# Graph attention on one core: data kept in the queries' order, and the tile of one-edge queries without q

## The chip, the cores and the metric

The kernel runs on one core of one Trainium2 chip. The time is device time in microseconds of that core, from runs of the whole program. A profiled execution, recorded separately, gives the span from the first to the last instruction and what each engine did. Engines are named as in the profile: PE (matmuls), PEld (weight loads of PE), DVE (vector), ACT (scalar), POOL (GpSimd), SP (sync). Gathers and scatters by rows are issued by POOL, plain loads and stores mostly by SP.

## The reference, cut to what matters

Sixteen batches of x (1024 x 512) go through one layer: masked attention with 8 heads of 64 over a fixed adjacency (1024 x 1024, the same in all batches), output projection, residual and layer norm. All is float32.

```
q, k, v = x @ Wq + bq, x @ Wk + bk, x @ Wv + bv        # 8 heads of 64
scores  = q . k / 8 + (1 - adj) * -1e9
attn    = softmax(scores)
out     = (attn @ v) @ Wo + bo
x       = layernorm(x + out)                            # no scale, no shift
```

The adjacency is sparse. A query with no edge gets the mean of all rows of v, since all its scores are shifted alike. A query with exactly one edge has a softmax over one key: its weight is 1, and its attention is that key's row of v.

## The kernel before

**Order by degree.** The function ranks counts the edges of every query, ranks the queries by that count (L395, eight comparisons of 128 x 1024) and scatters (query, count) to a DRAM table, order, by eight row scatters (scatter, L389). SP reads the table back as ranked; asked_row (L409) is the list of original query numbers in sorted order. Sorted queries form eight tiles of 128. The function edges then gathers each tile's rows of the adjacency (codes, L433), multiplies them by the key's number (L438, place), and takes the largest entries out as lists of keys (kl). From these it writes key_row: for each block, one key per query.

**Blocks.** Tile t has OWN[t] blocks in which each of its 128 queries has a key of its own, and BLOCKS[t] blocks that hold the remaining edges of its dense queries, summed by a matmul (add_up). There are NB = 29 + 6 = 35 blocks a batch, 560 in all.

**Fronts.** The products of x with the weights are called fronts: load_x brings a tile of x in (L548, on SP, three tiles ahead, three buffers), transpose_x turns it on PE (pxT, L555), pair projects two tiles to q (pq, four matmuls by product, L584) and to k and v by a scheme of seven products (x, pp, z, L698). All is kept in the natural order of rows: out_q (L614) scales q on DVE and stores it to q_rows, send stores k and v to kv_rows. Both tables exist three times, so that the batches in work do not meet.

**The attention of a block.** gather (L888 on) fetches q rows once per tile (qt, L894) and for the dense blocks qg (L904), and for each block the rows of k and v of its keys (kvg, L910, 128 rows of 4 KB), all by row gathers on POOL. products (L931) multiplies q by k on DVE, scores (L935) sums per head, exponentials (L945) is on ACT, weigh scales v, on ACT (L955, eight instructions) or on DVE (L959), add_own (L971) adds up, normalise (L999, L1000) divides, and the result is transposed on PE (poT, L1008). finish multiplies by Wo (po, L584), adds the residual row gathered from x (y, L752), normalises (a power on POOL, L820) and scatters the rows to their places in the output (L830).

**The order of the work** is written out by hand. A loop runs over steps n, one block each; step n issues products(n+4), exponentials(n+3), the gathers of block n+8, the weighting of a later block and so on, in a fixed order for every engine's queue. Functions given to later(k, ...) are issued k steps on. In each step PE also gets a share of fronts or of finish, by its costs (PRODUCT, SUM, TRANSPOSE), so that the fronts run more than a batch ahead. Thirty-four steps of lead-in come before block 0; in them ranks and edges run beside the fronts of batch 0 and 1. The attended rows of tiles 102 to 111 (SPILL) are stored and multiplied at the end. PSUM has four rotating banks (fill_psum) for pq, pxT, pp, po and poT.

A guard computes whether the assumptions on the counts and on the size of the scores hold; if not, tile_general runs the whole layer again.

Of the kernel before, what the change touches and what calls it, by code (L numbers as in the profile page):

```python
# [26 lines left out]
OWN = (1, 2, 2, 3, 4, 5, 5, 7)  # L27
# [4 lines left out]
KG_BUFS, Q_BUFS, PV_BUFS, Y_BUFS = 8, 7, 5, 6  # L32
NO_ROW = 65536.0

# [7 lines left out]
ROWS = 3  # L42
# [118 lines left out]
def kernel(  # L161
# [48 lines left out]
    own = [sum(OWN[:t]) for t in range(NT)]  # L210

# [17 lines left out]
    with ExitStack() as main:  # L229
# [16 lines left out]
        place = one.tile([P, N], F32, name="place")  # L246
        nc.gpsimd.iota(place, pattern=[[1, N]], base=1, channel_multiplier=0, allow_small_or_imprecise_dtypes=True)
# [15 lines left out]
        key_row = one.tile([P, NB], I32, name="key_row")  # L263
        query_row = one.tile([P, NS], I32, name="query_row")
# [9 lines left out]
        key, rank = (one.tile([P, NT], F32, name=name) for name in ("key", "rank"))  # L274
        rank_row, asked_row = (one.tile([P, NT], I32, name=name) for name in ("rank_row", "asked_row"))
        ADJ = []
# [12 lines left out]
        bias_rows = one.tile([2 * NPAIR, P], F32, name="bias_rows")  # L289
        bv_rows = one.tile([NPAIR, P], F32, name="bv_rows")  # L290

        def loads():
# [14 lines left out]
            for i in range(ROWS):  # L307
                nc.scalar.dma_start(kv_rows[i][N:N + 1, 0:D], zero)
            nc.vector.tensor_scalar(before, place[:, 0:P], -1.0, query[:, 0:1], op0=OP.add, op1=OP.is_gt)
# [40 lines left out]
        now, plan, rest, urgent = [0], {}, {}, []  # L350
# [9 lines left out]
        def ranks():  # L360
# [4 lines left out]
            zeros = small.tile([P, 2 * NT], F32, name="order_first", bufs=1)  # L365
            nc.gpsimd.memset(zeros, 0.0)
            nc.gpsimd.dma_start(order.rearrange("(p t) c -> p (t c)", p=P), zeros)
# [26 lines left out]
            for t in range(NT):  # L394
                nc.vector.scalar_tensor_tensor(  # L395
                    keys, row, key[:, t:t + 1], place, op0=OP.is_lt, op1=OP.min, accum_out=rank[:, t:t + 1]
                )
                if t:
                    nc.vector.tensor_copy(rank_row[:, t - 1:t], rank[:, t - 1:t])
                    scatter(t - 1)  # L400
                if t % 3 == 2:
                    yield
            nc.vector.tensor_copy(rank_row[:, NT - 1:NT], rank[:, NT - 1:NT])
            scatter(NT - 1)
            yield
            nc.sync.dma_start(ranked, order.rearrange("(t p) c -> p t c", p=P))
            yield
            yield
            nc.vector.tensor_copy(asked_row, ranked[:, :, 0])  # L409
            yield  # L410
            nc.vector.tensor_scalar(lone, ranked[:, 0, 1:2], 0.0, None, op0=OP.is_le)
# [16 lines left out]

        def edges(t):
# [8 lines left out]
            nc.vector.tensor_tensor(v, v, place, op=OP.mult)  # L438
            st = small.tile([P, 4], F32, name="est")
            deg, end, lim, off = (st[:, i:i + 1] for i in range(4))  # L440
            kl = small.tile([P, J + 2], F32, tag=f"kl{J}", name=f"kl_{t}", bufs=2 if J == 8 else 1)
            kr = small.tile([P, max(OWN)], F32, tag="kr", name=f"kr_{t}", bufs=2)
# [21 lines left out]
            if J > SEGMENT:  # L464
# [5 lines left out]
            nc.vector.tensor_scalar(off, kl[:, 0:1], 0.0, N + 1.0, op0=OP.is_le, op1=OP.mult)  # L470
            nc.vector.tensor_tensor(kl[:, 0:1], kl[:, 0:1], off, op=OP.add)

            rows, missing = kr[:, 0:K], absent[:, own[t]:own[t] + K]
            nc.vector.tensor_scalar(rows, kl[:, 0:K], -1.0, float(N), op0=OP.add, op1=OP.min)
            nc.vector.tensor_scalar(missing, rows, 0.0, None, op0=OP.is_lt)
            yield
            nc.vector.scalar_tensor_tensor(
                key_row[:, NS + own[t]:NS + own[t] + K], missing, NO_ROW, rows, op0=OP.mult, op1=OP.max
            )
# [13 lines left out]
            nc.vector.tensor_copy(kl[:, J + 1:J + 2], ranked[:, t, 0:1])  # L493
            nc.vector.tensor_tensor(end, off, deg, op=OP.add)
# [10 lines left out]
            step = min(nb, HALF // (J + 2))  # L505
            assert step * J <= D
            for i0 in range(0, nb, step):
# [3 lines left out]
                g = pg[:, 0:n * (J + 2)].rearrange("p (n j) -> p n j", n=n)  # L511
# [3 lines left out]
                e = small.tile([P, 2, n], F32, tag=f"ee{n}", name=f"ee_{t}_{i0}", bufs=2)  # L515
# [11 lines left out]
                nc.vector.tensor_tensor(key_row[:, g0:g0 + n], e[:, 1, :], e[:, 0, :], op=OP.max)  # L527
                nc.vector.tensor_copy(query_row[:, g0:g0 + n], g[:, :, J + 1])
# [16 lines left out]
        def load_x(b, t):  # L545
            if b < B:
                X[b, t] = work.tile([P, D], F32, tag="x", name=f"x_{b}_{t}", bufs=3)
                nc.sync.dma_start(X[b, t], x[b, ds(t * P, P), :])  # L548

        def transpose_x(b, t):  # L550
# [25 lines left out]
            return [(TRANSPOSE, pe, None)]  # L576

        def product(name, lhs, w, out):

            def unit(c):  # L580
# [3 lines left out]
                nc.tensor.matmul(p, lhs()[:, ts(c, P)], w[:, c, :], start=(c == 0), stop=(c == NPAIR - 1))  # L584
# [16 lines left out]
        def pair(b, j):  # L601
# [8 lines left out]
            def out_q(i, p):  # L610

                assert gathered[0] >= NB * (b - ROWS + 1)
# [44 lines left out]
            def lhs(i):  # L657
                return lambda: XT[b, tt[i]]

            q0, q1 = (product(f"pq_{b}_{tt[i]}", lhs(i), W["q"], lambda p, i=i: out_q(i, p)) for i in range(2))  # L660
# [118 lines left out]
        def finish(b, t):  # L779
# [92 lines left out]
            units = product(f"po_{b}_{t}", lambda: OT[b, t], W["o"], out)  # L872
# [10 lines left out]


        KG, QG, PV, PSUM, QT, RDEN = {}, {}, {}, {}, {}, {}
        blocks = [(b, t, i) for b in range(B) for t in range(NT) for i in range(OWN[t] + BLOCKS[t])]

        def gather(n):  # L888
            b, t, i = blocks[n]
# [326 lines left out]
```

## Time and profile before

| what | value |
|---|---|
| median of 3 runs | 1974.01 us (1973.77 to 1976.46) |
| span of the profiled execution | 1981.3 us |
| the profiled execution's own time | not given beside its span |
| busy PE, DVE, ACT, POOL | 1914.7, 1786.6, 1554.5, 1288.2 us |
| DMA | 563.10 MB, mean 284 GB/s |
| row gathers and scatters (software queue) | 403.22 MB, 61.9% of 16 engines' span |
| plain transfers of SP and ACT (main queue) | 153.16 MB, 20.9% |

Busy time of PE is the sum of records that overlap a little, so it is read together with the chain of waits. The chain goes back from the last instruction, at each step to whatever released it. A stage is a stretch of the span, given with the busy time of every engine in it. The groups give count, busy time and mean length per line; "idle before" names what ended the idle time of that engine.

### The profile page before, as it was taken

The page shows a single profiled execution, that of the slowest core. Times are in us where ns is not written, and L with a number is a line of the kernel's source. Part 1 is how long each engine was busy: PE and PEld are TensorE (multiplying, and loading weights), DVE is VectorE, ACT ScalarE, POOL GpSimd, SP SyncE. Part 2 cuts the span into 40 slices and gives each one's busy share as a digit, 9 for nine tenths or more (in the row PEclk, how much of TensorE's full clock was granted, in tenths as well). Part 3 has the DMA queues.
Part 4 walks back from the last instruction along what each step waited for, and adds up shares of the span by engine and source line. Part 5 has one row for each costly group of instructions (what it writes and reads, how often), then busy time and mean ns, then how long its engine had stood idle before and what let it go on. Part 6 is the DMA issues. An engine that isn't in the chain of part 4 may idle for free.

```text
span 1981.3 us, 25750 instructions
## 1 busy us (share of the span) xinstructions
PE 1914.7 (97%) x5375; PEld 923.3 (47%) x5375; DVE 1786.6 (90%) x3756; ACT 1554.5 (78%) x6096; POOL 1288.2 (65%) x1206
## 2 busy tenths in 40 slices
PE   8988999999999999999999999999999999999895
PEld 3434454444545454454544445454444545444442
DVE  2789999999899999999998999989899999999895
ACT  3525878878797887879888787879789798978785
POOL 1653565756667676767667586766757675566684
PEclk9999999999999999999999999999999999999998
DMA  6697887888879788888889788888978889998994
GB/s 250 214 339 253 265 303 246 301 280 273 315 262 318 253 303 287 299 296 270 306 255 319 269 290 285 298 303 262 312 260 290 293 291 321 313 316 269 324 313 154
DMA packets 191140, 563.10 MB, mean 284 GB/s; under 512 B 31711, under 2 KB 31739, under 8 KB 190974
## 3 DMA queue, kind: packets, MB, share of 16 engines
q0 software_dynamic: 121632, 403.22, 61.9%
q1 hardware_dynamic: 66736, 153.16, 20.9%
q10 hardware_dynamic: 2606, 4.99, 0.7%
q14 instruction: 122, 1.00, 0.2%
q8 instruction: 44, 0.72, 0.1%
HBM read 442.25 MB, written 143.71 MB: 296 GB/s over the span
## 4 chain that ended last, share of the span: by engine, by line
PE 75%; DVE 12%; issue 3%; ACT 2%; DMA 0%; POOL 0%; another core or an unknown queue 0%; DVEq 0%; POOLq 0%; ACTq 0%
PE po L584 19%; PE pq L584 17%; PE pp L698 13%; PE z L698 9%; PE x L698 9%; DVE qk L931 3%; DVE s L935 2%; PE poT L1008 2%; PE pxT L555 2%; PE sum L981 2%; PE sum L980 2%; ACT pv L955 1%; DVE pv L971 1%; PE pm L646 1%; DVE o L1000 1%
## 5 line engine op out<-in xcount | busy, mean ns | idle before, releaser
L910 POOL DMA_INDIRECT kvg<-kv_rows,key_row x560 | 629.5, 1124 | 435.0 <-ACT pv L945 111.6
L955 ACT ACTIVATE pv<-kvg,pv 128x64 f32<-128x64 f32 x3552 | 894.4, 338 | 0.0
L584 PE MATMUL pq<-wq,xT 128*128 128x512 f32 x1024 | 481.5, 600 | 2.0 <-issue 1.5
L584 PE MATMUL po<-wo,oT 128*128 128x512 f32 x944 | 436.7, 595 | 4.2 <-DVE y L804 1.9
L935 DVE TENSOR_REDUCE s<-qk 128x8 f32<-128x512 f32 x560 | 380.8, 680 | 6.0
L931 DVE TENSOR_TENSOR qk<-qt,kvg 128x512 f32<-128x512 f32 x464 | 317.4, 684 | 4.8 <-DMA kvg<-kv_rows,key_row 3.1
L584 PEld LDWEIGHTS pq<-wq,xT 128*128 128x128 f32 x1024 | 192.7, 193 | 223.2 <-issue 209.4
L584 PEld LDWEIGHTS po<-wo,oT 128*128 128x128 f32 x944 | 175.5, 191 | 206.1 <-issue 190.8
L698 PE MATMUL pp<-t,s 128*128 128x512 f32 x504 | 239.6, 598 | 9.5 <-DVE s L570 9.5
L698 PE MATMUL x<-b,xT 128*128 128x512 f32 x504 | 237.1, 593 | 0.0
L971 DVE TENSOR_TENSOR pv<-pv,pv 128x520 f32<-128x520 f32 x336 | 232.9, 693 | 0.0
L945 ACT ACTIVATE pv<-s,absent 128x8 f32<-128x8 f32 x464 | 135.3, 293 | 107.7 <-DVE s L935 69.2
L830 POOL DMA_INDIRECT out_dram<-y,asked_row x128 | 153.2, 1197 | 37.6 <-issue 26.1
L894 POOL DMA_INDIRECT qt<-q_rows,asked_row x128 | 139.8, 1092 | 36.8 <-issue 35.0
L594 ACT ACTIVATE sq_k<-kv 128x128 f32<-128x128 f32 x512 | 150.6, 299 | 10.0 <-DVE kv L721 9.0
L698 PEld LDWEIGHTS pp<-t,s 128*128 128x128 f32 x504 | 95.2, 191 | 119.1 <-issue 107.7
L698 PEld LDWEIGHTS x<-b,xT 128*128 128x128 f32 x504 | 94.6, 190 | 112.4 <-issue 109.0
L752 POOL DMA_INDIRECT y<-in_x_dram,asked_row x102 | 116.0, 1137 | 30.6 <-issue 30.0
L904 POOL DMA_INDIRECT qg<-q_rows,query_row x96 | 106.1, 1105 | 27.2 <-issue 25.3
L698 PE MATMUL z<-b,s 128*128 128x512 f32 x252 | 118.5, 592 | 0.7 <-DVE kv L726 0.7
L698 PE MATMUL pp<-t,xT 128*128 128x512 f32 x252 | 118.5, 593 | 0.1
L698 PE MATMUL z<-t,s 128*128 128x512 f32 x252 | 118.6, 593 | 0.0
(195 smaller groups left out, 2608.8 us busy)
## 6 DMA issues: line engine op xcount, KB each, us to landing
kv_rows<-kv SPq DMA_DIRECT2D x128, 512.0 KB
x<-in_x_dram SPq DMA_DIRECT2D x128, 256.0 KB
q_rows<-q SPq DMA_DIRECT2D x128, 256.0 KB
kvg<-kv_rows,key_row POOLq DMA_INDIRECT x560
residual<-y_sorted SPq DMA_DIRECT2D x26, 256.0 KB
y<-residual SPq DMA_DIRECT2D x26, 256.0 KB
adj<-in_adj_dram POOLq DMA_DIRECT2D x8, 512.0 KB
spill<-oT SPq DMA_DIRECT2D x10, 256.0 KB
```

The costliest lines, as they stand in the source:

```text
L584: nc.tensor.matmul(p, lhs()[:, ts(c, P)], w[:, c, :], start=(c == 0), stop=(c == NPAIR - 1))
L594: nc.scalar.activation(sq, s[:, ts(h, P)], AF.Square, scale=scale, accum_out=sums[:, h:h + 1])
L698: nc.tensor.matmul(R[bank], l[:, ts(c, P)], right[:, c, :], start=(first and c == 0), stop=(c == 1), skip_group_check=True,)
L752: nc.gpsimd.indirect_dma_start(out=y, out_offset=None, in_=x_rows, in_offset=bass.IndirectOffsetOnAxis(ap=asked_row[:, t:t + 1], axis=0), ...
L830: nc.gpsimd.indirect_dma_start(out=out_rows[b, t], out_offset=bass.IndirectOffsetOnAxis(ap=asked_row[:, t:t + 1], axis=0), in_=y, in_offse ...
L894: nc.gpsimd.indirect_dma_start(out=QT[b, t], out_offset=None, in_=q_rows[b % ROWS], in_offset=bass.IndirectOffsetOnAxis(ap=asked_row[:, t: ...
L910: nc.gpsimd.indirect_dma_start(out=KG[n], out_offset=None, in_=kv_rows[b % ROWS], in_offset=bass.IndirectOffsetOnAxis(ap=key_row[:, g:g + ...
L931: nc.vector.tensor_tensor(QK[n], q, KG[n][:, 0:D], op=OP.mult)
L935: nc.vector.tensor_reduce(S[n], QK.pop(n).rearrange("p (h d) -> p h d", d=HD), axis=AX.X, op=OP.add)
L945: nc.scalar.activation(PV[n][:, D:], S.pop(n), AF.Exp, bias=bias)
L955: nc.scalar.activation(pv[:, ts(h, HD)], v[:, ds(D + h * HD, HD)], AF.Copy, scale=pv[:, D + h:D + h + 1])
L971: nc.vector.tensor_tensor(PV[b, t], PV[b, t], pv, op=OP.add)
```

## The change

The sorted order, until now only that of the attention, becomes the order of all tables from batch 1 on. load_x gathers the rows of x by asked_row on POOL instead of loading them on SP; so k, v and q of batches 1 to 15 are stored sorted, and a tile of q is read back by a plain load on SP. Batch 0 is projected in the natural order, as the order is not known in time, and has index lists of its own (key_row0, query_row0). As the keys are sorted as well, the lists need each key's sorted place: the multiplier of the adjacency rows is a code (2048 times the place, plus the number), made by ranks from the ranks and spread over the partitions by eight more transposes on PE. decode takes it apart again by four small operations.

The ranks are moved: places 64 to 191 become tile 1, the places below 64 and those from 192 to 255 become tile 0. In the adjacency given, 60 queries have no edge and 141 have one, so tile 1 holds queries with exactly one edge. It has no block: its single key's row of v is gathered (v1, half as wide as kvg) and goes to the transpose in place of the normalised sum. Tile 0 now has two blocks, so there are 28 + 6 = 34 blocks for a batch in which steps are counted (NBT), 544 in all. For batches 1 to 15 no q is projected for tile 1. Buffers move: seven qt buffers become four (qg and v1) and three (qs, for tiles of q).

```diff
-OWN = (1, 2, 2, 3, 4, 5, 5, 7)
+OWN = (2, 1, 2, 3, 4, 5, 5, 7)
...
-KG_BUFS, Q_BUFS, PV_BUFS, Y_BUFS = 8, 7, 5, 6
+KG_BUFS, Q_BUFS, QT_BUFS, PV_BUFS, Y_BUFS = 8, 4, 3, 5, 6
+CODE, ROUND = 2048.0, 12582912.0
+LONE, ONE_KEY = 64, 1
...
             for t in range(NT):
                 nc.vector.scalar_tensor_tensor(
-                    keys, row, key[:, t:t + 1], place, op0=OP.is_lt, op1=OP.min, accum_out=rank[:, t:t + 1]
+                    keys, row, key[:, t:t + 1], place[:, 0:1].to_broadcast([P, N]), op0=OP.is_lt, op1=OP.min, accum_out=rank[:, t:t + 1]
                 )
-                if t:
-                    nc.vector.tensor_copy(rank_row[:, t - 1:t], rank[:, t - 1:t])
-                    scatter(t - 1)
                 if t % 3 == 2:
                     yield
-            nc.vector.tensor_copy(rank_row[:, NT - 1:NT], rank[:, NT - 1:NT])
-            scatter(NT - 1)
+            for at, by in ((LONE, LONE), (LONE + P, -LONE - P), (2 * P, P)):
+                nc.vector.tensor_scalar(key, rank, float(at), float(by), op0=OP.is_ge, op1=OP.mult)
...
+            nc.vector.tensor_tensor(rank, rank, moved, op=OP.add)
+            nc.vector.tensor_copy(rank_row, rank)
+            for t in range(NT):
+                scatter(t)
             yield
             nc.sync.dma_start(ranked, order.rearrange("(t p) c -> p t c", p=P))
...
+            nc.vector.scalar_tensor_tensor(key, rank, CODE, key, op0=OP.mult, op1=OP.add)
+            nc.vector.tensor_copy(keys.rearrange("p (t q) -> p t q", t=NT), key[:, :, None].to_broadcast([P, NT, P]))
+            yield
+            pk = [fill_psum(f"pcodes_{i}") for i in range(2)]
+            for t in range(NT):
+                nc.tensor.matmul(pk[t // 4][:, ts(t % 4, P)], keys[:, ts(t, P)], ident, start=True, stop=True)
...
+                nc.scalar.copy(CODE_OF[i], pk[i])
             nc.vector.tensor_copy(asked_row, ranked[:, :, 0])
             yield
+            known.append(True)
...
+        def decode(code, high):
+            nc.vector.tensor_scalar(high, code, 0.5 - CODE / 2, 1.0 / CODE, op0=OP.add, op1=OP.mult)
+            nc.vector.tensor_scalar(high, high, ROUND, None, op0=OP.add)
+            nc.vector.tensor_scalar(high, high, -ROUND, None, op0=OP.add)
+            nc.vector.scalar_tensor_tensor(code, high, -CODE, code, op0=OP.mult, op1=OP.add)
...
-            nc.vector.tensor_tensor(v, v, place, op=OP.mult)
+            for i in range(2):
+                nc.vector.tensor_tensor(v[:, ts(i, HALF)], v[:, ts(i, HALF)], CODE_OF[i], op=OP.mult)
...
+            decode(rows, high)
+            nc.vector.scalar_tensor_tensor(key_row[:, g:g + K], missing, NO_ROW, high, op0=OP.mult, op1=OP.max)
+            nc.vector.scalar_tensor_tensor(key_row0[:, g:g + K], missing, NO_ROW, rows, op0=OP.mult, op1=OP.max)
...
         def load_x(b, t):
             if b < B:
+                if b and not known:
+                    waiting.append((b, t))
+                    return
                 X[b, t] = work.tile([P, D], F32, tag="x", name=f"x_{b}_{t}", bufs=3)
-                nc.sync.dma_start(X[b, t], x[b, ds(t * P, P), :])
+                if b:
+                    gather_x(X[b, t], b, t)
+                else:
+                    nc.sync.dma_start(X[b, t], x[b, ds(t * P, P), :])
...
+            q0, q1 = (
+                product(f"pq_{b}_{tt[i]}", lhs(i), W["q"], lambda p, i=i: out_q(i, p)) if b == 0 or tt[i] != ONE_KEY else []
+                for i in range(2)
+            )
...
-        blocks = [(b, t, i) for b in range(B) for t in range(NT) for i in range(OWN[t] + BLOCKS[t])]
+        blocks = [(b, t, i) for b in range(B) for t in range(NT) if t != ONE_KEY for i in range(OWN[t] + BLOCKS[t])]
...
         def gather(n):
             b, t, i = blocks[n]
+            if t == ONE_KEY + 1 and i == 0:
+                g = NS + own[ONE_KEY]
+                V1[b] = work.tile([P, D], F32, tag="qt", name=f"v1_{b}", bufs=Q_BUFS)
+                nc.gpsimd.indirect_dma_start(
+                    out=V1[b], out_offset=None, in_=kv_rows[b % ROWS],
+                    in_offset=bass.IndirectOffsetOnAxis(ap=keys_of(b)[:, g:g + 1], axis=0), element_offset=D,
+                )
             if i == 0:
-                tag, bufs = ("qt", Q_BUFS) if fronts or t % 2 else ("x", 3)
+                tag, bufs = ("qs", QT_BUFS) if fronts or t % 2 else ("x", 3)
                 QT[b, t] = work.tile([P, D], F32, tag=tag, name=f"qt_{b}_{t}", bufs=bufs)
-                nc.gpsimd.indirect_dma_start(
-                    out=QT[b, t], out_offset=None, in_=q_rows[b % ROWS],
-                    in_offset=bass.IndirectOffsetOnAxis(ap=asked_row[:, t:t + 1], axis=0),
-                )
+                if b:
+                    nc.sync.dma_start(QT[b, t], q_rows[b % ROWS][ds(t * P, P), :])
+                else:
+                    gather_q(QT[b, t], b, asked_row[:, t:t + 1])
...
-            return 0 < i < OWN[t] or n < total - NB and (n % 2 == 0 or n < NB // 2)
+            return 0 < i < OWN[t] or n < total - NBT and (n % 2 == 0 or n < NBT // 2)
...
+                if 0 <= n < total and blocks[n][1:] == (ONE_KEY + 1, 1):
+                    turn(blocks[n][0], ONE_KEY, V1.pop(blocks[n][0]))
```

For the two tiles with dense queries (6 and 7) the lists of the shared blocks get the same decoding and a second set of query numbers. The new function turn is the former end of normalise: transpose, copy and hand-over. Elsewhere NB becomes NBT, and place shrinks to 640 columns.

## The prediction

> **What bounds the kernel now.** I read the page first, then the stages, then the chain, since an average hides which engine binds where.
>
> ```profile
> span 1981.3 us, 25750 instructions
> ...
> PE 1914.7 (97%) x5375; PEld 923.3 (47%) x5375; DVE 1786.6 (90%) x3756; ACT 1554.5 (78%) x6096; POOL 1288.2 (65%) x1206
> ```
>
> ```profile
> 100.00:150.00 50.00, 43.45 (x109) 18.73 (x108) 43.33 (x124) 11.89 (x50) 29.68 (x29) 0.97 0.96 341
> 150.00:200.00 50.00, 43.87 (x129) 21.17 (x128) 45.80 (x110) 29.92 (x121) 15.37 (x16) 0.93 0.73 253
> ...
> 500.00:1000.00 500.00, 499.02 (x1422) 243.94 (x1422) 467.64 (x958) 412.33 (x1645) 348.76 (x320) 1.00 0.86 290
> ...
> 1700.00:1800.00 100.00, 90.86 (x260) 43.80 (x260) 98.14 (x185) 85.45 (x358) 60.99 (x55) 0.98 0.89 306
> ```
>
> In the stages, the columns after the length are busy time of PE, PEld, DVE, ACT and POOL, then clock, DMA share, GB/s. In mid-run PE has no gap and DVE has 6.5% to spare. From 1700 us it turns round: DVE 98, PE 91. From 100 to 200 us neither is full; each waits for the other. A busy PE alone proves little, so the chain of work from 500 to 1000 us, and three of its pieces:
>
> ```profile
> by line: PE pq L584 23.2%; PE po L584 22.7%; PE pp L698 17.2%; PE z L698 11.3%; PE x L698 11.3%; PE poT L1008 3.1%; PE pxT L555 2.8%; PE sum L981 2.2%; PE sum L980 2.2%; DMA kvg<-kv_rows,key_row 1.9%; PE pm L646 0.8%; issue 0.3%; DVE s L935
> ...
> 556.86 3.43 PE pq L584 x8
> 562.01 3.43 PE po L584 x8
> 571.03 3.43 PE po L584 x8
> ```
>
> The chain is PE for about 97%, so a product taken off PE here is time off the run. The price of a q tile is the piece: eight records, 3.43 us (0.43 us each), not the 600 ns mean of its row. The mean of a batch: the first and last mean L646 start at 117.6 and 1843.9 us, 15 batches, 115.1 us each.
>
> **What the Trainium skill says.** "Perfetto Trace Analysis", Identifying the Most-Contended Engine: matmul busy time misjudges PE, because matmuls are pipelined. The trace agrees: rows of 600 ns follow each other every 430 ns. The same page, DMA Instruction, SWDGE: the record of a GpSimd DMA ends when its descriptors are made, not when the data is there. It agrees: the kvg record takes 1.12 us, while a kvg transfer stands in the chain with 9.36 us. "DMA: Bandwidth & Descriptors", Issuing engines are not separate DMA queues: transfers from SP and POOL share the same 16 engines. So swapping plain and gathered loads between these queues buys no bandwidth. "VectorE: DVE Perf Modes", the errata section: each SBUF operation pays a fixed latency, so small ones are dear. Here 128x1 takes 145 ns (L817) against 682 ns for 128x512.
>
> **The change part by part.**
>
> 1. *No q for tile 1 in batches 1 to 15.* Fifteen products of 3.43 us leave PE, 51.5 us in all. Batches 2 to 14 are projected while PE binds, which counts in full: 13 x 3.43 = 44.6. Batch 1's falls in the DVE-paced set-up (0.6 us, its DVE part), batch 15's after 1727 us (the last-but-one mean), where DVE binds. DVE loses 15 q of 0.68, SP 15 stores.
>
> 2. *One block fewer per batch* (35 to 34; tile 0 takes two, tile 1 none). DVE loses per batch the product 0.684, the score 0.680, one weighting (0.686; seven to six by the parity rule), the reciprocal 0.193, the scaling o 0.694; with q 0.682 that is 3.62 us. ACT loses one exponential (0.29); its 28 weightings stay. DVE goes from 107.7 (0.936 x 115.1) to 104.1 of the new 111.7 us: it keeps the same slack, and PE remains the bound. Where DVE binds, this is itself the gain: 3.1 for the 0.87 batch between 1700 and 1800, 2.9 for the last batch (no q in it), 1.5 for half of the first: 7.5 us.
>
> 3. *Gathers.* POOL drops 121 of the 128 qt gathers and issues 120 x gathers; 544 kvg and 16 half-width v gathers replace 560 kvg. POOL's count and its 69% are unchanged. SP drops 120 x loads and gets 105 q loads. Their landing is not shown; as blocks are gathered eight ahead and multiplied four ahead, they have four steps of 3.3 us. DVE's waits for kvg total 3.1 us over 560 blocks, so such transfers are covered now; I take zero, with 0 to 10 us for the q loads held behind stores on SP. Traffic falls by 0.75 MB a batch, 2% of 35 MB. V's transposes cost PE what o's did.
>
> 4. *Where x now waits.* An x gather waits for a PE transpose to free one of three x buffers, and POOL is in order, so the kvg gathers, the row scatters and the power of the statistics stand behind it. SP shows the price today:
>
> ```profile
> SPq L548 <- PE pxT L555: 109.0, 43, 7.0
> ```
>
> That is 109 us in 43 waits. What covers it: POOL itself idles 435 us ahead of kvg gathers, mostly waiting for ACT to free kvg buffers. Bounds 0 and 109; I take 0.
>
> 5. *The set-up*, where the change adds. The order is now scattered only after all ranks are known and moved:
>
> ```profile
> 48.94 1.33 POOL L389 DMA_INDIRECT order<-asked,rank_row  x1 [37.11 <-DVE rank_row L399]
> ...
> 60.08 0.96 POOL L389 DMA_INDIRECT order<-asked,rank_row  x1 [0.30 <-issue]
> ...
> 67.41 0.28 DVE L409 CAST asked_row<-ranked 128x8 int32<-128x8 f32 x1 [2.83 <-DMA ranked<-order]
> 67.49 0.69 DVE L614 SCALAR_TENSOR_TENSOR q<-pq,bq_bc 128x512 f32<-128x512 f32 x1
> ```
>
> Ranks end at 57.7 us; less seven casts (0.8), plus eight dependent small operations (0.165 each, as L470 to L475 take 0.66 for four): 58.2. Eight scatters 1.3 us apart end at 68.5 instead of 61.0, so asked_row comes at 74.9 instead of 67.4. Queued behind it on DVE is the read of pq tile 4, and its bank is the one that the transpose of x tile 7 needs (four banks: pq, pb, pp, pxT, then pxT). PE reaches that at 69.5 + 1.8 (the added transposes of the codes, as pkeys took) = 71.3, and DVE frees it at 75.6: a stall of 4.3 us. PE is 6.1 us late. Behind the scatters on POOL come x of batch 1 and the adjacency gathers, about 8 us later too. x of batch 1 is due at 92 us and lands near 86 (at the 9.36 above): covered. Then the decoding: five more small operations for each of eight tiles (40 x 0.165 = 6.6) and seven for each of tiles 6 and 7 (2.3), with 0.3 for split products: 9.2 us on DVE between 95 and 190 us, where it idles 11 of 100. I let 6 of it through (bounds 0 and 9). Together +12.1 us (bounds 4 and 18). The scatter of batch 0's order, the zero rows and the smaller tables lie beside idle queues: nothing.
>
> **Sum**, against the profiled execution: -44.6 - 7.5 - 0.6 + 12.1 = -40.6. The page gives the span alone, and nothing lies around it that I can read: 1981.3 - 40.6 = 1940.7. The median of the runs is 1974.01, 0.9963 of that span, so 1934.
>
> **The rivals.**
>
> *POOL is held by x* (the slower side). If the 109 us of waits move from SP to POOL and come through to DVE, the span is 1940.7 + 109 = 2050, in runs 2042. It decides from 40.6 us on, 0.34 us for each of 120 gathers. For it: DVE has only 7 us a batch to catch up. Against it: the idle time of POOL before kvg, and four steps between a gather and its use.
>
> *Half given back*: queues and sequences on SP and POOL leak 20 to 35 us, landing at 1955 to 1968. For it: DMA at 0.86, four qt buffers where seven were (the fifth qg of tile 7 must await a product of its own step).
>
> *Set-up dear or free*: +18 or +4 instead of +12.1 gives 1940 or 1926.
>
> *DVE becomes the bound*: then the gain is DVE's 3.6 a batch instead of PE's 3.43, and the time the same; so it is not a separate case in time.
>
> *The tile is not what the change says*: if a query of ranks 64 to 191 had not one edge, the guard would run the general version, far above 2042. The adjacency given has 60 queries without an edge and 141 with one, so ranks 64 to 191 all have one. Excluded.
>
> **How the numbers follow.** The forecast with its set-up bounds (1926 to 1940, or somewhat beyond from PE's own pace) gets 0.70; half given back 0.15; POOL held 0.09; a deeper gain, with the set-up hidden and DVE's tail worth more, 0.06. Predicted 1934. The range 1920 to 1957 leaves out the slower case, the upper part of the second, and a little below. A measurement of this kernel can tell about 0.2% (4 us) from no change. Faster 0.88, within 0.03, slower 0.09.
>
> **What would show it right or wrong.** Right: pq with 904 records instead of 1024 at the same 0.43 us pace; PE full from 200 to 1650 us with means of a batch 111.7 apart; asked_row near 75 us with PE waiting at the transpose of x tile 7; the first kvg gather some 10 us later than 126 us. Wrong: POOL waiting for PE pxT by tens of us with DVE qk waiting for kvg or qt; PE gaps in mid-run; batches still 115 apart.

## The result, and the profile after

| what | before | after |
|---|---|---|
| median of 4 runs | 1974.33 us (1973.77 to 1976.46) | 1982.71 us (1981.95 to 1984.58) |
| ratio | 1 | 1.0039, 95% interval 1.0025 to 1.0053 |
| profiled execution | span 1981.3 us | 1981.95 us, span 1980.2 us |

The changed kernel is slower by 0.4%, where 2% faster was forecast, and a ratio of 1 lies outside the interval. Around a span lie some 1.8 us. So the profiled execution of before, 1981.3 + 1.8 us, was about 9 us longer than its typical run, and the two spans must not be compared with each other. Where stretches of mid-run are compared below, a second trace of before is used (e5_before, span 1975.2 us); the set-up, the end and the waits just below are read in the first.

The page of the changed kernel, and four of its stages (columns as in the prediction):

```profile
span 1980.2 us, 25432 instructions
...
PE 1878.0 (95%) x5271; PEld 904.0 (46%) x5271; DVE 1746.8 (88%) x3727; ACT 1544.4 (78%) x6074; POOL 1282.8 (65%) x1206
```

```profile
100.00:150.00 50.00, 38.45 (x87) 15.99 (x86) 46.95 (x154) 9.47 (x40) 30.00 (x31) 0.90 0.91 311
150.00:200.00 50.00, 44.70 (x134) 21.30 (x133) 46.79 (x136) 26.00 (x112) 21.49 (x22) 1.00 0.83 277
500.00:1000.00 500.00, 491.14 (x1406) 239.37 (x1405) 457.23 (x938) 414.61 (x1661) 343.99 (x321) 1.00 0.84 285
1700.00:1800.00 100.00, 89.13 (x255) 43.13 (x254) 93.56 (x175) 85.46 (x357) 58.09 (x50) 0.97 0.86 301
```

The work did leave PE and DVE: both are busy 37 to 40 us less over the run. But the run did not get shorter, so the work left holes behind. The first and last mean (L691) start at 125.8 and 1841.4 us, so batches come 114.4 us apart, not 115.1, but far from 111.7. In mid-run PE, without a gap before, now stands for 8.9 of 500 us; from 100 to 150 us it is busy 38 instead of 43, at a clock of 0.90. The chain from 500 to 1000 us, some 97% PE before, is now cut up:

```profile
by line: PE po L629 15.8%; PE pq L629 13.7%; PE pp L746 10.3%; PE z L746 8.3%; PE x L746 7.9%; issue 5.0%; DMA kvg<-kv_rows,key_row 5.0%; DVE qk L991 3.8%; ACT pv L1015 3.7%; DVE s L995 3.1%; PE poT L1074 2.3%; PE pxT L600 2.0%; PE sum L104
```

The waits from 200 to 1700 us say who waited for whom (us in all, times, longest). First the changed kernel, then the first of these in the kernel before, where the second stood at 11.7:

```profile
ACT oT L1078 <- PE po L629: 97.8, 26, 7.4
...
DVE stats L865 <- ACT ysq L862: 54.0, 26, 4.9
...
POOL x L800 <- PE pxT L600: 23.9, 17, 4.4
```

```profile
ACT oT L1012 <- PE po L584: 34.4, 18, 3.3
```

oT is the copy that ACT makes of a tile's turned attention (poT, out of PSUM), but what ACT waited for is po, the product with Wo. The timeline around one such wait, of a tile 2, shows how that is to be read (start, length, engine, line, operation; in brackets the idle time before it):

```profile
1000.76 0.60 PE L1074 MATMUL poT<-ident,o 128*128 128x128 f32 x4
1001.20 1.88 PE L746 MATMUL pp<-t,xT 128*128 128x512 f32 x4
...
1002.92 1.88 PE L746 MATMUL z<-b,s 128*128 128x512 f32 x4
1004.64 3.60 PE L629 MATMUL po<-wo,oT 128*128 128x512 f32 x8
...
1008.27 0.59 ACT L1078 COPY oT<-poT 128x512 f32<-128x512 f32 x1 [7.26 <-PE po L629]
1008.75 2.02 ACT L1015 ACTIVATE pv<-kvg,pv 128x64 f32<-128x64 f32 x8
...
1015.45 1.12 PE L629 MATMUL po<-wo,oT 128*128 128x512 f32 x2 [1.63 <-DVE y L852]
```

The transpose that ACT copies was done at 1001.4 us. The copy starts at 1008.27, when po of an earlier tile ends at 1008.24. As po reads an oT buffer, the reading is that ACT was waiting for that buffer, not for data. Behind the copy on ACT stand the weighting pv and the square ysq; DVE then waits for ysq (stats), and at 1015.45 PE waits for DVE. That is a theory from one picture, which the experiments test.

### The profile page after: what moved, and what is told of

It is laid out like the page before. It is cut to its first block, busy times and chain, and to the rows that moved or that the text cites. A ratio compares the mean times of both kernels' runs of the same rounds, so it can differ in the third digit from the quotient of the medians.

```text
span 1980.2 us, 25432 instructions
## 1 busy us (share of the span) xinstructions
PE 1878.0 (95%) x5271; PEld 904.0 (46%) x5271; DVE 1746.8 (88%) x3727; ACT 1544.4 (78%) x6074; POOL 1282.8 (65%) x1206
## 4 chain that ended last, share of the span: by engine, by line
PE 58%; DVE 19%; ACT 6%; issue 5%; DMA 3%; POOL 1%; POOLq 0%; DVEq 0%; ACTq 0%
PE po L629 15%; PE pq L629 12%; PE pp L746 9%; PE z L746 7%; PE x L746 7%; DVE qk L991 4%; ACT pv L1015 4%; DVE s L995 4%; DMA kvg<-kv_rows,key_row 2%; PE poT L1074 2%; DVE pv L1031 2%; PE pxT L600 2%; PE sum L1040 2%; PE sum L1041 2%; DVE y L853 1%
## 5 line engine op out<-in xcount | busy, mean ns | idle before, releaser
L970 POOL DMA_INDIRECT kvg<-kv_rows,key_row x544 | 622.0, 1143 | 388.5 <-ACT pv L1005 118.1
L629 PE MATMUL pq<-wq,xT 128*128 128x512 f32 x904 | 426.9, 599 | 4.8 <-DVE y L852 2.4
L995 DVE TENSOR_REDUCE s<-qk 128x8 f32<-128x512 f32 x544 | 370.4, 681 | 6.9
L991 DVE TENSOR_TENSOR qk<-qt,kvg 128x512 f32<-128x512 f32 x448 | 306.9, 685 | 13.0 <-DMA kvg<-kv_rows,key_row 12.9
L629 PEld LDWEIGHTS pq<-wq,xT 128*128 128x128 f32 x904 | 168.5, 192 | 194.3 <-issue 174.9
L1005 ACT ACTIVATE pv<-s,absent 128x8 f32<-128x8 f32 x448 | 131.0, 294 | 66.7 <-DVE s L995 65.6
L800 POOL DMA_INDIRECT x<-in_x_dram,asked_row x120 | 128.9, 1074 | 78.7 <-PE pxT L600 42.5
L878 POOL DMA_INDIRECT out_dram<-y,asked_row x128 | 148.9, 1163 | 36.4 <-issue 20.5
L1078 ACT COPY oT<-poT 128x512 f32<-128x512 f32 x128 | 73.8, 577 | 104.8 <-PE po L629 99.0
```

What stands on the lines that cost most here:

```text
L629: nc.tensor.matmul(p, lhs(c), w[:, c, :], start=(c == 0), stop=(c == NPAIR - 1))
L800: nc.gpsimd.indirect_dma_start(out=y, out_offset=None, in_=x_rows, in_offset=bass.IndirectOffsetOnAxis(ap=asked_row[:, t:t + 1], axis=0), ...
L878: nc.gpsimd.indirect_dma_start(out=out_rows[b, t], out_offset=bass.IndirectOffsetOnAxis(ap=asked_row[:, t:t + 1], axis=0), in_=y, in_offse ...
L970: nc.gpsimd.indirect_dma_start(out=KG[n], out_offset=None, in_=kv_rows[b % ROWS], in_offset=bass.IndirectOffsetOnAxis(ap=keys_of(b)[:, g:g ...
L991: nc.vector.tensor_tensor(QK[n], q, KG[n][:, 0:D], op=OP.mult)
L995: nc.vector.tensor_reduce(S[n], QK.pop(n).rearrange("p (h d) -> p h d", d=HD), axis=AX.X, op=OP.add)
```

## The experiments

Each group ran on one chip together with the kernel before, and ratios are to before on that chip (1% is 19.7 us). The theories: **A**, the oT stall, either as a missing buffer (A1) or as a transpose late in PE's queue (A2), since tiles 0, 1 and 2 now end in three steps following each other. **B**, x gathers on POOL hold up the key gathers (B1: because they wait there for PE; B2: because a gather costs more than a load). **C**, with 34 blocks, an even number, the parity rule of by_act gives ACT the same blocks in every batch.

### First group: one part at a time

Its chip ran the kernel before at 1995.62 us (1986.2 to 2002.6), 1% above the others, and the changed kernel was not run there. So these four are compared with each other, and by their traces.

*e1_v1_late*

```diff
-                if 0 <= n < total and blocks[n][1:] == (ONE_KEY + 1, 1):
+                if 0 <= n < total and blocks[n][1:] == (ONE_KEY + 4, 2):
```

> The changed kernel with one line moved: the transpose of v1 (the gathered row of v of tile 1) is handed over at the third block of tile 5 instead of the second block of tile 2, so that no other tile ends near it. Theory A (bunched tile ends: tiles 0, 1 and 2 end in three consecutive steps of a batch, PE's transposes for them queue behind po and the fronts, ACT waits 5 to 7 us at the copy oT of tile 2 in each batch, then DVE for ACT, then PE for DVE): the wait of ACT oT for PE falls from 98 us to under 50, PE's gaps in mid-run close, batches come 112.0 to 112.8 us apart instead of 114.4, and the time falls by 25 to 38 us, to about 1945 to 1957. Theory B (x gathers on POOL delay the key gathers) and theory C (the same pattern of weightings on ACT in every batch, since 34 blocks are an even number): no change, 1979 to 1986.

Measured: 1977.34 us, ratio 0.9915 (0.9888 to 0.9943). ACT's wait for po at oT is gone from the list, and stats waits 14.7 us for ysq instead of 54. So the waits that A links go together. But from 500 to 1600 us PE still stands 1.4 us a batch, and batches come 113.7 us apart where A expected 112.0 to 112.8. A is not all, and A1 and A2 are not told apart.

*e2_alt*

```diff
-            return 0 < i < OWN[t] or n < total - NBT and (n % 2 == 0 or n < NBT // 2)
+            return 0 < i < OWN[t] or n < total - NBT and ((n + b) % 2 == 0 or n < NBT // 2)
```

> The changed kernel with the parity of the weightings that ACT takes alternating by batch, (n + b) % 2 instead of n % 2, as it alternated by itself with 35 blocks. Theory C: the long runs of ACT weightings no longer meet the same steps in every batch, and half or more of the 40 us come back: 1940 to 1962. Theory A: ACT waits at the copy of tile 2 whatever it weighs next; within 6 us of the changed kernel, 1977 to 1988. Theory B: no change either.

Measured: 2015.01 us, ratio 1.010 (1.0071 to 1.0128). C expected 1940 to 1962. ACT still waits 100.5 us for po at oT, and PE stands 41 us from 500 to 1600 us, against 19 in the changed kernel and in e3. C is refuted: the alternation gives nothing back, and it harms.

*e3_plain_x*

```diff
-                if b:
-                    gather_x(X[b, t], b, t)
-                else:
-                    nc.sync.dma_start(X[b, t], x[b, ds(t * P, P), :])
+                nc.sync.dma_start(X[b, t], x[b, ds(t * P, P), :])
```

> The changed kernel with x of batches 1 to 15 loaded plainly on SP, in the natural order, at the same places of the program (so the rows no longer match the sorted lists; the amount of work is the same). Theory B (POOL's order: kvg, scatters and powers behind x gathers that wait for PE): POOL's 42 us of waiting for the transposes of x goes, key gathers start earlier, and the time falls by 15 us or more, to under 1967. Theory A: the waits of POOL are covered by its idle time; within 5 us, 1977 to 1987.

Measured: 1981.45 us, ratio 0.9933 (0.9908 to 0.9957). ACT still waited 96 us for po, and the steps at the stall are as long as ever. Without the changed kernel on that chip the gain of B cannot be read off; left open here.

*e4_q_all*

```diff
-                product(f"pq_{b}_{tt[i]}", lhs(i), W["q"], lambda p, i=i: out_q(i, p)) if b == 0 or tt[i] != ONE_KEY else []
+                product(f"pq_{b}_{tt[i]}", lhs(i), W["q"], lambda p, i=i: out_q(i, p))
```

> The changed kernel with q projected and stored for tile 1 in all batches, though nothing reads it: the first step of the prediction undone alone. If PE were still the bound, as predicted, +45 to +51 us: 2027 to 2033. Theory A: PE has 2 us of gaps in every batch, but they lie in a few steps and a product is spread by the share of PE over the batch, so most of the 3.43 us comes back as time: +25 to +45, 2007 to 2027. If PE were slack: under +15.

Measured: 2038.68 us, ratio 1.0224 (1.0196 to 1.0253), the slowest of the four and above every case that was expected. It is 57 us over e3, more than the 51.5 us of the products themselves, and PE stands 25 us from 500 to 1600 us, so the product that came back did not fill the holes. Why it cost more than its length was not traced. The skipped product is worth having; what it is worth without the stalls is settled by e16.

### Second group: the buffer

*e5_before* and *e6_after* are the two kernels, unchanged.

> The kernel before, unchanged, for a trace from the chip on which the next three run. Without the buffer stall that theory A puts into the changed kernel, its mid-run batches stand 114 to 116 us apart with PE gaps under 0.3 us a batch, and ACT waits under 40 us for po at the copy oT. Ratio to itself 1.000.

> The changed kernel, unchanged, on the same chip, as the base for the next two. As measured first: 1.002 to 1.005 of the kernel before. If the chip of the earlier four experiments was one that slows the kernel before more than the changed one, this can be under 1. Mid-run batches 113.5 to 114.5 us apart, PE gaps of 1.5 to 2.5 us a batch, 90 to 105 us of ACT waiting for po at the copy oT.

Measured: 1979.15 us, ratio 1.0004 (0.9995 to 1.0014), and 1989.76 us, 1.0059 (1.004 to 1.0077): slower than before, as on the first chip.

*e7_oT5*

```diff
-                    OT[b, t] = work.tile([P, D], F32, tag="oT", name=f"oT_{b}_{t}", bufs=LAZY + 2)
+                    OT[b, t] = work.tile([P, D], F32, tag="oT", name=f"oT_{b}_{t}", bufs=LAZY + 3)
```

> The changed kernel with five buffers for oT (the turned attention of a tile) instead of four, and nothing else. Theory A1 (what ACT waits for at the copy of tile 2 is a free oT buffer: tiles 6 and 7 of the batch before and 0 and 1 of this one hold all four until po of tile 6 is done): the wait of ACT oT for PE po falls from 98 us to under 25, the block in which it stood from 6.5 to about 3.8 us, and the time by 20 to 40 us. Theory A2 (the transpose itself is late in PE's queue, since three tiles end in three steps): the wait stays, now named for poT, and the time within 5 us of the changed kernel.

Measured: 1968.66 us, ratio 0.9948 (0.9929 to 0.9967): 21 us faster than the changed kernel, and faster than before. ACT no longer waits for po at all; it waits 14 us for the transpose itself, in short pieces:

```profile
ACT oT L1078 <- PE poT L1074: 14.1, 14, 2.1
```

The block in which the stall stood takes 3.9 us instead of 6.5. Only a buffer was added and no instruction moved, so **A1 is shown** and A2 falls. The four buffers were held by tiles 6 and 7 of the batch before and 0 and 1 of this one; tile 2 had to wait for po of tile 6. The trace of the changed kernel agrees: in each of batches 1 to 12 the copy of tile 2 starts 0.04 us after the end of po of the tile four copies earlier, which is that tile 6. "Perfetto Trace Analysis" in the Trainium skill, Optimization Strategy, says that the same gap coming back on the engine that should be full can mean too few buffers for the next tile. It is so here, two engines removed: the buffer is ACT's, the gap PE's.

*e8_oT5_v1*: e7 and the edit of e1.

> Five oT buffers and the later hand-over of v1 (third block of tile 5) together. Theory A1: one remedy is enough, within 5 us of five buffers alone. Theory A2: the hand-over does the work, so it is as fast as with the hand-over alone and 20 us or more faster than five buffers alone.

Measured: 1967.01 us, ratio 0.9932 (0.991 to 0.9954), the same as e7. One remedy is enough, as A1 says.

The stage from 500 to 1600 us shows what is left. Before (e5_before), the changed kernel (e6_after), five buffers (e7_oT5):

```profile
500.00:1600.00 1100.00, 1100.00 (x3124) 535.47 (x3123) 1032.51 (x2116) 912.87 (x3634) 760.45 (x701) 1.00 0.86 288
```

```profile
500.00:1600.00 1100.00, 1078.95 (x3067) 523.05 (x3066) 1000.90 (x2055) 908.88 (x3621) 751.39 (x700) 1.00 0.83 282
```

```profile
500.00:1600.00 1100.00, 1089.18 (x3096) 529.50 (x3095) 1015.95 (x2086) 925.83 (x3678) 765.01 (x710) 1.00 0.84 285
```

PE stands 0, 21 and 11 us: the buffer closed about half of it. The half is rough, as e9 below, whose mid-run work is that of e7, stands 15.5.

### Third group: the set-up, and x again

*e9_early* is e7 with

```diff
+                nc.vector.tensor_copy(rank_row[:, t:t + 1], rank[:, t:t + 1])
+                scatter(t)
...
-            nc.vector.tensor_copy(rank_row, rank)
-            for t in range(NT):
-                scatter(t)
...
-            nc.sync.dma_start(ranked, order.rearrange("(t p) c -> p t c", p=P))
+            nc.sync.dma_start(ranked[0:LONE, 0, :], order[0:LONE, :])
+            nc.sync.dma_start(ranked[LONE:P, 0, :], order[LONE + P:2 * P, :])
+            nc.sync.dma_start(ranked[:, 1, :], order[LONE:LONE + P, :])
+            nc.sync.dma_start(ranked[:, 2:, :], order[2 * P:, :].rearrange("(t p) c -> p t c", p=P))
```

> Five oT buffers, and the order scattered as in the kernel before, tile by tile while the ranks are still being counted, by the ranks as they come; the moving of places 64 to 191 is done by the reading side, four loads of parts of the table instead of one. The result is the same. If the set-up loses what the prediction said by the late order (asked_row 8.4 us later, PE waiting 5.1 us for DVE at the transpose of x tile 7): asked_row at 66 to 69 us instead of 74.0, that wait of PE gone, the first product of batch 0 some 6 to 8 us earlier than with five buffers alone, the ratio to the kernel before 0.003 to 0.004 lower, at 0.990 to 0.992. If DVE's lists between 100 and 200 us set the pace whatever came before: under 2 us, ratio 0.994 to 0.995.

Measured: 1963.25 us, ratio 0.9916 (0.9889 to 0.9943), 6.3 us better than e7 by the ratios of two chips, though the intervals overlap. The trace shows the step itself: asked_row at 65.2 us instead of 74.0, no wait of PE for DVE at the transpose of x, and the first product of batch 0 at 149.1 us instead of 155.9. What is left in mid-run:

```profile
500.00:1600.00 1100.00, 1084.47 (x3086) 526.86 (x3085) 1011.46 (x2080) 920.73 (x3661) 757.23 (x707) 1.00 0.84 284
```

*e10_early_plx*: e9 and the edit of e3.

> The one before (five oT buffers, early order) with x of batches 1 to 15 loaded plainly on SP in the natural order (the rows no longer match the sorted lists; the amount of work is the same). Theory B, on top of the buffer: x gathers on POOL wait for PE and hold up key gathers, and this is the remaining PE gap of 1.4 us a batch: 10 to 25 us faster than the one before. Theory A1 alone: POOL has idle time to cover them, within 5 us of it.

Measured: 1945.61 us, ratio 0.9841 (0.9817 to 0.9865): 15 us faster than e9. PE stands 3.8 us from 500 to 1600 us instead of 15.5. **B is right** about what was left; B1 and B2 are not told apart yet.

*e11_nodec*: e9 with decode left out.

```diff
-            decode(rows, high)
...
-                decode(e[:, 1, :], e[:, 2, :])
```

> Five oT buffers, early order, and no decoding: the codes hold the query's number alone, so the four operations of decode are left out in each of ten places and the lists of the batches after the first hold natural numbers (wrong rows, the same number of gathers). Forty operations of 0.15 to 0.17 us, 6 to 6.5 us of DVE between 100 and 200 us. If DVE paces this stage, as its 94 of 100 us says: 5 to 7 us faster than with early order alone; if only two thirds came through, as predicted: 4 us; if PE paces it: under 2 us.

Measured: 1954.21 us, ratio 0.9887 (0.9863 to 0.9912), 5.7 us below e9 with overlapping intervals. That is the size of the prediction's 6 us, but it does not show that decode costs it. The first product of batch 0 starts no earlier (149.4 us against 149.1), and mid-run, where no decode is left, is faster too: batches 3 to 13 come 112.3 us apart instead of 113.4. The lists hold other rows, so the gathers are not the same, and what decode costs stays open.

*e12_early_v1*: e9 and the edit of e1.

> Five oT buffers, early order and the later hand-over of v1, all three: the version that theory A1 and the set-up step would build, 0.988 to 0.992 of the kernel before. Against early order without the hand-over: within 5 us (A1: the buffer is the cause and one remedy enough), or 5 to 10 us faster, most of it in batches 0 to 2, as the trace of the hand-over with five buffers hinted (blocks 0 of batch 0 to 3: 347 us there against 355).

Measured: 1963.91 us, ratio 0.9917 (0.9896 to 0.9938), as e9.

### Fourth group: why x costs

*e13_late_x*: e9, and each gather asked for two steps later.

```diff
-                    load_x(n // NT, n % NT)
+                    later(2, lambda: load_x(n // NT, n % NT))
```

> Five oT buffers and early order, with each x gather issued two steps later (about 6.7 us), when the transpose that frees its buffer is done. Theory B1 (the gather waits on POOL for PE, 33 us in 21 waits, and what stands behind it on POOL is late): the waits of POOL for pxT fall under 8 us and most of the 15 us by which plain loads of x were faster come back, 0.9835 to 0.987 of the kernel before. Theory B2 (the price is the gather itself: 120 more transfers in the row queue ahead of the key gathers, with 1 us of POOL each): within 5 us of the unmoved gathers, 0.989 to 0.994.

Measured: 1945.78 us, ratio 0.9860 (0.9844 to 0.9877), 11 us faster than e9 by the ratios of two chips, as fast as the plain loads of e10. The wait for pxT is gone from POOL's list; PE is nearly full again (3.7 us of 1100 are missing, 15.5 in e9), in the stage from 500 to 1600 us and in the chain from 500 to 1000 us:

```profile
500.00:1600.00 1100.00, 1096.34 (x3126) 534.21 (x3124) 1025.57 (x2105) 930.62 (x3707) 765.57 (x717) 1.00 0.85 288
```

```profile
by line: PE po L631 23.4%; PE pq L631 21.3%; PE pp L748 17.2%; PE x L748 12.4%; PE z L748 11.7%; PE poT L1076 3.2%; PE pxT L602 2.8%; PE sum L1043 2.6%; PE sum L1042 2.5%; ACT pv L1017 0.8%; PE pm L693 0.8%; issue 0.2%; ACT ysq L864 0.1%; A
```

The gathers are all still there, so **B1 is shown** for the changed kernel, with e15 below as a second way: what cost was not the gather but the place where its issue waited in POOL's order. "DMA: Bandwidth & Descriptors" in the Trainium skill, Anatomy of one DMA, says that DMA engines do not wait on semaphores, and the issuing sequencer does so before dispatch. Here POOL stood 42.5 us for pxT over the whole of the changed kernel (55.4 in e9), with everything behind it.

*e14_before_gx*: the kernel before, with

```diff
+                if b > 1:
+                    gather_x(X[b, t], b, t)
+                else:
+                    nc.sync.dma_start(X[b, t], x[b, ds(t * P, P), :])
```

> The kernel before with one part of the change alone: x of batches 2 to 15 gathered on POOL by the sorted list instead of loaded on SP (112 gathers; the rows no longer match, the work is the same; the q gathers stay on POOL too, so POOL has 112 issues more). Step 4 of the prediction put this at 0. Theory B: 15 to 30 us slower, 1.007 to 1.015. If the x gathers harm only together with what else the change does: within 4 us of 1.

Measured: 1991.49 us, ratio 1.0088 (1.0072 to 1.0104): 17 us slower, from this part alone. The waits from 300 to 1650 us name what was late on POOL, the power of the statistics first:

```profile
DVE stats L826 <- POOL stats L823: 43.0, 21, 4.8
DVE qk L934 <- DMA kvg<-kv_rows,key_row: 17.5, 13, 3.6
POOL x L755 <- PE pxT L558: 12.9, 11, 2.0
```

In e5_before the first stood at 4.0 us in 3 waits and the second at 1.2. This kernel also has 112 more issues on POOL, which is busy for 1414.9 us instead of 1291.0. So e14 shows what x gathers cost on a POOL that keeps its other gathers, and does not tell the wait from the added work.

*e15_x4*: e9 with four x buffers, and the edit of e1 in place of the fifth oT buffer.

> Early order and the later hand-over of v1 (which takes the place of the fifth oT buffer, since there is no room for both), and four x buffers instead of three, each gather still asked for three tiles ahead: so it never waits for the transpose that was just issued. B1: as with the gathers two steps later, 0.9835 to 0.987. B2: as with three buffers, 0.989 to 0.994.

Measured: 1946.94 us, ratio 0.9866 (0.9847 to 0.9885), as e13. POOL's wait for pxT falls from 33.1 to 6.1 us from 300 to 1650 us. Two ways to take the wait away, one gain.

*e16_q_all*: e9 and the edit of e4.

> Five oT buffers and early order, with q projected and stored for tile 1 in every batch: what the skipped product is worth once the buffer stall is gone. Step 1 of the prediction: 15 products of 3.43 us, 44.6 to 51.5 us, a ratio of 1.014 to 1.018 against 0.9916 without. If the stalls hide part of it, 25 to 40 us, 1.004 to 1.012.

Measured: 1982.42 us, ratio 1.0045 (1.0031 to 1.0059), 25 us slower than e9, and 36.5 us slower than e13. With the product back, PE stands 0.4 us in 1100, though POOL waits 52 us for pxT from 300 to 1650 us. So in this kernel the wait of POOL costs PE nothing, and it costs 11 us once the product is gone. That the room left by the product makes the wait show fits both; no run tests it further, and e14 warns against a rule, as PE had been just as full there.

```profile
POOL x L802 <- PE pxT L602: 52.0, 23, 4.8
```

```profile
500.00:1600.00 1100.00, 1099.59 (x3125) 535.85 (x3124) 1007.99 (x2063) 908.10 (x3614) 753.17 (x696) 1.00 0.84 283
```

### Fifth group: the sum, and the best version

*e18_late_only*: the changed kernel with the edit of e13 alone.

> The changed kernel with the later x gathers alone; four oT buffers and the late order stay. If the losses add up: 8 to 15 us better than the changed kernel, a ratio of 0.997 to 1.001. If the buffer stall of 2.7 us in every batch sets the pace and hides the wait of POOL behind it: under 4 us, 1.002 to 1.006.

Measured: 1976.44 us, ratio 1.0017 (1.001 to 1.0024), against 1.0039 and 1.0059 of the changed kernel on other chips: 4 to 8 us, between the two expectations. The stall at oT still takes 96 us of ACT and seems to hide part of the other loss; so the losses do not simply add up.

*e17_best*: e13 and the edit of e1.

> The changed kernel with all that helped: five oT buffers, the order scattered early, each x gather two steps later, and the later hand-over of v1. Against the same without the hand-over (0.986 of the kernel before): within 4 us, as the hand-over and the fifth buffer answer the same stall, so 0.984 to 0.988. If the shorter first batches of the two runs with the hand-over are its own gain, up to 7 us better, 0.982.

Measured: 1942.04 us, ratio 0.9842 (0.9828 to 0.9855). It is 31 us faster than the kernel before, and close enough to e13 that the later v1 has no clear gain of its own. With the three small edits of e13 (buffer, early order, later x gathers) the change gains 28 us and lands inside the forecast range, some 12 us short of the 40 that were forecast; as it stands, it loses.

## Why the prediction was wrong, point by point

Two terms that the prediction put at nothing ate the gain: step 3 saw no cost in where v1 goes, and step 4 priced the wait of x on POOL at 0. The two gains were also too large. The sum, with each part by the difference of two ratios; by their intervals, each difference is good to some 4 to 6 us. The last row is what is left of the +11.6 us of e6_after.

| part | predicted | measured | from |
|---|---|---|---|
| no q (1) | -45.2 us | -36.5 us | e13 against e16 |
| oT buffer (3) | not seen | +21.9 us | e6 against e7 |
| x waiting on POOL (4) | 0 | +11.1 us | e9 against e13 |
| set-up, one block fewer, all else (5, 2) | +4.6 us | +15 us | the rest |

The order in which parts are undone matters: x's wait gave 11 us back without the oT stall and 4 to 8 with it (e18).

**Step 1, no q: right in kind, too large.** pq has 904 records, as foreseen. Once both stalls are gone, batches come 111.7 us apart (first products of batches 3 and 13 of e13), the very spacing that was named. That is luck: the 115.1 from which 3.43 us were taken off was a mean of all 15 batches, those near the set-up among them. By batches 3 to 13 the same trace takes 114.4, the second trace of before 114.2 and e16, with q, 114.4. So a batch gains 2.8 us. Of the missing 0.7 us, 0.3 are PE's remaining gaps; PE's busy time falls by 3.1 us a batch and not by 3.43, and that rest is not explained.

**Step 2, one block fewer: the slack was right, the gain at the end is not there.** DVE has 7.6 us of slack a batch in e13, 6.9 before. But the stretch from the last mean to the end, 137.4 us before, takes 138.4 after. From 1700 to 1800 us DVE fell from 98 to 93.6 and PE from 90.9 to 89.1. Neither is full, and the likely reading, which no run tests, is that the end is paced by their waits for each other. No run undoes this part alone, but the traces show none of its 7.5 us.

**Step 3, gathers: one sentence of it holds the largest mistake.** "V's transposes cost PE what o's did" priced the transpose and not the place where its result goes. v1 is ready as soon as it is gathered, and is handed over in the step between the ends of tiles 0 and 2. As tile 0 has two blocks now and tile 1 none, tile 2 ends four steps after tile 7 of the batch before; in the kernel before it was five, and four buffers were almost enough. The wait was already there, 34.4 us in 18 pieces, and the prediction did not read it. The key gathers were covered less well than step 3 had it: DVE waits 14.1 us for kvg from 200 to 1700 us instead of 3.1. The plain q loads and the fewer qt buffers were not tried by themselves. SP's waits for qs buffers, 21 us for DVE and 17 for ACT, are on no chain that was read, and stand in e13 too (25 and 18), where PE is nearly full.

**Step 4, x on POOL: the wait that was named, priced at nothing, costs 11 us.** The cover named was POOL's 435 us of idle time ahead of key gathers. That is an average: it says that POOL has time, not that it has time then. Nor is it "mostly" waiting for ACT, which ended 220 of the 435 us. The power of the statistics, for which DVE came to wait 43.0 us in e14, had no cover there. Of the 109 us in which SP waited, 42.5 became POOL's.

**Step 5, the set-up: right in its steps, near in size.** asked_row came at 74.34 us (74.9 predicted), and PE stood at the transpose of x tile 7:

```profile
74.34 0.17 DVE L434 CAST asked_row<-ranked 128x8 int32<-128x8 f32 x1 [9.81 <-DMA ranked<-order]
74.42 0.69 DVE L659 SCALAR_TENSOR_TENSOR q<-pq,bq_bc 128x512 f32<-128x512 f32 x1
...
75.17 1.11 PE L600 MATMUL pxT<-ident,x 128*128 128x128 f32 x4 [5.45 <-DVE q L659]
```

That is 5.45 us for 4.3. The first key gather moved from 126.1 to 136.8 us. The first product of batch 0 moved from 143.1 to 155.9, by 12.8 us for 12.1; on the chip of the second group it came 14 us (e7) and 18 us (e6) after that of e5_before. How much of it is the decoding is open (e11).

**The rivals.** The one that came nearest was the first: POOL held by x, with its point of decision at 40.6 us of waits brought through. It held 11. "Half given back" had some of the size and, as far as the runs show, the wrong causes. The only buffers that it named were those of qt. None named oT, and that is why the range missed: no case of the forecast held a stall in every batch that the change makes by itself.

## What to carry to other kernels

When a change moves the moment at which tiles end, list every buffer on the path of a finished tile and count how many are held at once; the price of an instruction says nothing of it. A wait of a copy for a product that it does not read points to a buffer, and one more buffer, or a later hand-over, is the test. An issue that must wait for a buffer is best put into a queue that is worked in order after the point at which that buffer is free: here two steps later sufficed, and 11 us came back.

## What the runs showed of the hardware that was not expected

Chips differ by more than the effect: the kernel before took 1995.62 us on one and 1973 to 1979 us on five others, one occasion each.

After some gaps of 2 to 3 us PE runs at half its pace for a few us. With five oT buffers (e7_oT5) twelve products from 500 to 1640 us start 0.86 us after the one before, twice the usual 0.43. They follow three gaps, of 1.9 us (for which the trace names no cause), 2.1 and 3.2 us, and the granted clock is 0.59, 0.50 and 0.52 in the stretches 1059.2 to 1062, 1174.7 to 1177.2 and 1634 to 1638.5 us. After a gap of 2.0 us at 756 us it stays at 1.00, so the length of the gap alone does not decide. In the kernel before there is no such product. An estimate from these figures: the twelve cost 5 us (12 x 0.43) beside some 14 us of gaps, so a gap can cost more than its own length.
